# A Mamba block and a mixture of experts on one core: scans 1024 wide in SBUF, the carried state as a leading column, lighter norms, three more PSUM banks, and the order of the work as a written list

## The chip, the core and the metric

The kernel runs on one core of one Trainium2 chip. A core has five engines with a queue each: PE (TensorE, matrix products into PSUM), DVE (VectorE), ACT (ScalarE), POOL (GpSimd) and SP (SyncE, which only issues DMAs here). They work side by side and wait for one another by semaphores. SBUF is the working memory of 128 partitions; PSUM has eight banks of 2 KB per partition, and PE writes only there. POOL can't reach PSUM. The metric is the device time of one execution in microseconds.

## What is computed

The input x has 4 sequences of 512 tokens with 256 channels. Cut to what matters:

```python
x = x + layernorm(mamba(layernorm(x)))
x = x + layernorm(moe(layernorm(x)))

# mamba: 512 inner channels, 16 states each
xs, gate = split(h @ in_proj.T)
xt = silu(conv4(xs) + conv_b)                    # causal, per channel
ts, B, C = split(xt @ x_proj.T)
dt = softplus(ts @ dt_proj.T + dt_b)
for t in range(512):                             # per sequence
    state = state * exp(dt[t] * A) + dt[t] * B[t] * xt[t]
    y[t] = (state * C[t]).sum(states)
out = ((y + xt * D) * silu(gate)) @ out_proj.T

# moe: a shared part of 512 and 16 experts of 128 hidden channels; weights of the top 4
cw = top4(softmax(h @ w_router)), made to sum to 1
moe = sum over e of cw[e] * (silu(h @ we1[e]) * (h @ we3[e])) @ we2[e]
out = shared / 5 + moe * 4 / 5
```

All is float32.

## The kernel before, in words

**Tiling.** The tokens are worked on in units of U = 256, so there are 8 units, two to a sequence (`UB` = 2). Even units begin a sequence, odd units go on with the state that the even one left in the tile `carry`.

**The Mamba part of a unit.** `front` (L655) makes the norm, the transposition, the input product, the convolution (by matmuls), B and C, dt and u = dt * xt, and the gate. dt and u go to DRAM and come back by DMA as `rep` so that a partition holds one (channel, state) pair: 32 channels times 4 states fill 128 partitions, CG = 4 groups of channels make 128 channels (a c of 4), SG = 4 groups of states make 16. B and C come back as `bt` and `ct`. The recurrence runs in slots, numbered by k; a slot handles NJ = 2 groups of channels of one (c, g), 512 columns, so that a unit has 32 slots (`SLOTS`) and the kernel 256:

- `exps` (L523, ACT): two activations of 256 columns write exp(dt * A) into a PSUM tile `h` of one bank (three banks rotate); a copy from `zero` (L532) clears the first column of the second group, so that one scan can run through both without carrying state over.
- `inputs_of` (L534, POOL): `dbx` = u * B, 1024 columns for two slots at once (L541). In odd units a small addition (L543) puts the carried state times the first decay into the first column of each group; that term comes from `decay0` (POOL, L811), `decay1` (ACT, L814) and `delta` (POOL, L818).
- `scan` (L820, DVE): `tensor_tensor_scan` over 512 columns (L824), from `h` (PSUM) and `dbx` (SBUF) into `h`.
- `times_c` (L828, DVE): `hc` = h * C into SBUF (L832), a ring of 11.
- `keep` (L834, ACT): in even units the last column of each group is copied into `carry` (L836).
- `sum_y` (L838, PE): matmuls with `sel` sum over states into the PSUM tile `y`, four slots at a time; `close` (DVE, L858) and `gated_y` (POOL, L864) finish y.

**The expert part of a unit.** `chain` (L918) makes the output product, the norms, the residual and the routing weights. `experts` (L1129) goes through 10 blocks of two experts (the shared part counts as four): `hidden` (PE, L1088) twice into the PSUM tiles `h1` and `h3`, `act` (ACT, L1095 to L1100), `gated` (DVE, L1107, from th in SBUF and h3 in PSUM), `weighted` and `product` (POOL, L1103 and L1110, both operands in SBUF), `down` (PE, L1123, into `po`). The profile shows the PSUM tiles h, h1 and h3 all as "h".

**Norms.** `stats_of` (L374) is one `bn_stats` on DVE; `rstd_of` (L380) is four small POOL instructions (L383 to L386); `normalize` (L389) is two ACT instructions.

**PSUM.** Eight banks: three for the states h, and one each for f, y, h1, h3 and po.

**The order of the work.** Every step is added as a task to `Plan` with an engine, a planned duration, a rank, its dependencies and the buffers that it takes and uses. `Plan.order` (L212) simulates the engines' queues and picks at each point the task that can start soonest, or one of lower rank within the task's patience. SHIFTS, PATIENCE and NUDGES move ranks. The list that comes out is the order in which each engine's queue, SP's DMAs too, is filled. Where PE would idle before the first `down`, `warm` (L346) fills it with products of `ident` (L349).

Of the kernel before, what the change touches and what calls it, by code (L numbers as in the profile page):

```python
# [14 lines left out]
P = 128  # L15
# [19 lines left out]
NJ = 2  # L35
CP = CG // NJ
CSL = SG * CP
SLOTS = CI * CSL
YS = 2 * CP
# [11 lines left out]
    tail=4, bt=2, ct=2, xg=2, rep=3, delta=3, h=3, dbx=3, hc=11, yg=2, o=1, xn2=1, xn_t2=2, lg=2,  # L51
    cw=2, cw_t=1, w13=3, w2=4, cwb=4, th=2, g=3, q=2, res=1, f=1, y=1, h1=1, h3=1, po=1,
# [4 lines left out]
SHIFTS = dict(  # L57
    fA=(-2, -14.75, -1.5, -59.5, 52, 5.75, 37.75, 15),
    fB=(20.5, -5, 12.5, 6.25, 26.25, 45.25, 0, -46),
    fC=(7.75, 2, -31, -1.5, 13.5, 14, -33.5, 18),  # L60
    fD=(12, 34.75, 16.5, 0.25, -2.5, 39.25, 8, 11.25),
    exps=(5.75, 36.5, 17.25, -3.75, -60, 51.75, 2, 37.75),
    dbx=(6.5, 1.25, -27.75, -13.5, -14.25, 5.25, 14.25, 46.5),
    scan=(33.75, 18.75, -5.75, 40.75, 52.75, 51.5, 57.25, -15.75),
    hc=(-4.75, -60, 50.25, -27, 28.5, 59.25, 16.75, 26.75),
    keep=(58, 0, -5.75, 0, 52, 0, 14.5, 0),
    sum=(60, -12.75, 1.25, 31.25, 16.5, 7, 0.5, -43.25),
    close=(-4.75, 27.5, 5.5, -13.75, -3, 20, 15, 36.5),
    ld=(1.5, 29.25, 27, -3, 15.75, -7.5, 57.5, -5.25),
    bc=(5, 3, 5.25, 6, 10.5, 15.75, 0.75, -3.25),  # L70
    chain=(-26, -5.25, -55, -60, -6, -38.25, -22.75, 0.25),
    load=(-5.5, 34, -50.25, 21.25, -21.25, -44, 2.75, 5.5),
    h1=(45.5, 3, -35.75, 8.25, 25.75, -0.5, 14.75, 34.5),
    h3=(11.25, -3, -53.5, -26, -29.25, -19, -15.75, -4),
    act=(-6.25, 40.25, 5.5, -11.5, -31.5, 0, 0, -3.25),
    gated=(-2, -9.5, -4.5, -23.25, 11.75, -60, -3, 0),
    prod=(33, -50, 58.75, -60, -50.75, -26.25, -8.75, 0),
    down=(-18.75, 25.5, -45, 42.25, -60, -14, 0.75, 37),
    fin=(14.75, -3, 27.75, 59, 0.5, 59.5, 3.5, -4),
)  # L80

PATIENCE = dict(
    fA=(1.5, 0.1, 0.1, 0.3, 0.1, 1, 0.3, 0.1),
    fB=(2.2, 0.1, 0.1, 0.3, 0.1, 2.2, 0.6, 0.6),
    fC=(0.3, 0.1, 0.3, 1, 0.1, 0.6, 0.3, 0.3),
    fD=(2.2, 0.1, 0.1, 0.1, 0.1, 0.1, 0.1, 0.6),
    exps=(0.1, 0.1, 0.6, 0.1, 1.5, 0.3, 1.5, 0.3),
    dbx=(0.1, 0.3, 0.1, 0.1, 0.1, 0.1, 1, 1.5),
    scan=(0.1, 0.1, 0.1, 0.6, 0.1, 0.1, 0.1, 0.1),
    hc=(0.1, 0.1, 0.6, 1.5, 2.2, 0.1, 2.2, 0.1),  # L90
    keep=(0.1, 0.1, 0.1, 0.1, 0.6, 0.1, 0.1, 0.1),
    sum=(2.2, 0.1, 0.1, 0.1, 2.2, 0.1, 0.1, 0.1),
    close=(0.1, 0.1, 0.6, 1, 0.3, 0.3, 0.6, 1.5),
    ld=(1.5, 0.3, 1.5, 0.3, 0.1, 0.1, 0.1, 1.5),
    bc=(0.6, 0.1, 0.1, 1, 1, 0.1, 0.1, 0.3),
    chain=(0.6, 0.6, 0.1, 0.6, 0.6, 1, 0.1, 2.2),
    load=(2.2, 1, 0.6, 1, 2.2, 2.2, 0.6, 0.1),
    h1=(0.3, 0.3, 0.3, 0.1, 0.1, 0.1, 0.3, 0.1),
    h3=(0.1, 0.3, 2.2, 0.1, 0.1, 1, 0.6, 0.1),
    act=(0.6, 2.2, 0.1, 0.3, 0.1, 0.1, 0.6, 2.2),  # L100
    gated=(0.6, 0.3, 1, 0.1, 0.6, 0.1, 0.1, 1),
    prod=(2.2, 0.1, 0.1, 0.1, 0.1, 0.3, 0.1, 1.5),
    down=(0.1, 0.1, 0.1, 1.5, 0.1, 0.3, 0.1, 0.3),
    fin=(0.3, 0.3, 0.1, 1.5, 0.1, 1, 1, 0.3),
)

NUDGES = {
    ("gin", 0, 0): 5.5, ("pad0", 1, 0): 5.75, ("in", 1, 0): 3, ("xg", 1, 0, 1): 8,
    ("inputs", 1, 0): 8, ("gate", 1, 0): 14.5, ("evict", 2): 16.5, ("conv", 2, 1): -5.5,
    ("inputs", 2, 0): -27.75, ("pad0", 3, 1): -8, ("conv", 3, 1): 19.25, ("silu", 3, 1): -21.25,  # L110
    ("conv", 4, 0): 25, ("xg", 4, 0, 1): 7.5, ("gin", 4, 1): -27, ("gsig", 4, 1): 18.25,
    ("gate", 4, 1): 9.75, ("x_proj", 5): -1, ("in", 6, 1): -19.75, ("stats", 7): 5.5,
    ("conv", 7, 1): -22.5, ("x_proj", 7): 9.5, ("gin", 7, 0): 12.5, ("dbx", 2): -10,
    ("keep", 6): -14.25, ("keep", 9): -3, ("hc", 11): -1.75, ("keep", 11): -2.5,
    ("keep", 13): 13, ("dbx", 8): 32.75, ("keep", 16): -12, ("keep", 20): -21.25,
    ("scan", 21): 7, ("close", 6): -6, ("decay0", 7): -5, ("sum", 14): -3, ("yg", 7): -0.5,
    ("reps", 10): 12.5, ("hc", 84): 12.75, ("exps", 95): 10, ("exps", 96): -6.25,
    ("scan", 99): -7.75, ("sum", 24): -3, ("decay0", 13): 9.5, ("scan", 106): -3,
    ("sum", 27): -10, ("scan", 112): -14.75, ("scan", 118): 62, ("scan", 122): -3.5,
    ("scan", 125): -6.25, ("scan", 126): 2, ("scan", 138): -8.75, ("keep", 140): -4.75,  # L120
    ("scan", 144): 2.25, ("keep", 146): 27.25, ("scan", 157): 5.75, ("scan", 162): 23.25,
    ("dbx", 84): -4.75, ("decay0", 22): 4.5, ("scan", 179): 53.75, ("dbx", 91): 8.75,
    ("yg", 22): 57, ("scan", 196): -17.5, ("scan", 201): -0.25, ("reps", 26): 6,
    ("scan", 210): 11.25, ("scan", 214): -9, ("scan", 217): 6, ("sum", 54): 3.25,
    ("dbx", 110): -13, ("scan", 223): -8, ("delta", 28): 8.5, ("yg", 28): 24.5,
    ("scan", 235): -2.75, ("close", 29): 8, ("scan", 246): 48.75, ("scan", 252): -1.25,
    ("out0", 0): 35.5, ("rstd2", 0): -27.5, ("w13", 2): -3.75, ("cwb", 2): 15.75,
    ("h3", 3): 26.5, ("w13", 5): 14.75, ("product", 5): -7, ("w2", 6): -15, ("w13", 7): 4,
    ("gated", 7): -2, ("cwb", 9): 19, ("frstd", 0): -20.75, ("fadd", 0): 9.75,
    ("turnw", 1): 8.25, ("w13", 10): -12, ("h1", 10): 11.5, ("act", 15): -17.75,  # L130
    ("weighted", 17): -31.75, ("h3", 18): 3, ("down", 25): 17.75, ("cwb", 26): 10.75,
    ("down", 28): -9, ("h1", 29): -12.75, ("h1", 31): 8, ("down", 33): -14.5,
    ("act", 37): 15.25, ("add1", 4): 13.5, ("act", 46): -14.5, ("w13", 48): 9.5,
    ("share", 5): -10.75, ("cwb", 53): -4, ("h3", 54): 19, ("cwb", 54): -27.5,
    ("down", 54): -5.75, ("w2", 55): 2, ("h1", 55): -5, ("w2", 56): 2.5, ("w2", 58): 16,
    ("cwb", 59): -7.25, ("add1", 6): 8, ("down", 63): 15, ("h1", 67): -13.5, ("h1", 79): 3.25,
    ("fstats", 7, 1): -5, ("fadd", 7, 0): 8.75,
}

GROUPS = dict(  # L140
    fA=(1, "x stats rstd norm transpose evict"),
    fB=(1, "pad0 in tail conv sigmoid silu xg0"),
    fC=(1, "x_proj ssm store_bc dt softplus inputs rep"),
    fD=(1, "gin gsig gate xg1"),
    exps=(SLOTS, "exps"),
    dbx=(SLOTS // CP, "dbx"),
    scan=(SLOTS, "scan"),
    hc=(SLOTS, "hc"),
    keep=(SLOTS, "keep"),
    sum=(SLOTS // YS, "sum"),  # L150
    close=(CI, "close yg"),
    ld=(CI, "reps loadxg decay0 decay1 delta"),
    bc=(1, "bc"),
    chain=(1, "xr out0 out stats1 rstd1 norm1 add1 stats2 rstd2 norm2 turn2 evict2 router pads logits "
           "exp choose chosen total share turnw weigh store_cw"),
    load=(NB, "w13 w2 cwb"),
    h1=(NB, "h1"),
    h3=(NB, "h3"),
    act=(NB, "act"),
    gated=(NB, "gated"),  # L160
    prod=(NB, "weighted product"),
    down=(NB, "down down2"),
    fin=(1, "fin fstats frstd fmean fnorm fadd fstore"),
)
GROUP_OF = {kind: (g, per) for g, (per, kinds) in GROUPS.items() for kind in kinds.split()}


def shift_of(name):
    kind = name[0] + str(name[2]) if name[0] == "xg" else name[0]
    g, per = GROUP_OF[kind]  # L170
    n = name[1] // per
    return SHIFTS[g][n] if g in SHIFTS else 0.0, PATIENCE[g][n] if g in PATIENCE else 0.1


class Plan:
# [22 lines left out]
    def add(self, name, eng, dur, rank, fn, deps=(), alloc=(), uses=(), kb=0, done=None):  # L198
        shift, patience = shift_of(name)
        rank += shift + NUDGES.get(name, 0.0)  # L200
        t = dict(
            name=name, eng=eng, dur=dur, rank=rank, fn=fn, deps=[self.names[d] for d in deps],
            alloc=alloc, kb=kb, done=done, at=len(self.tasks), patience=patience,
        )
        assert name not in self.names, name
        self.names[name] = t
        self.tasks.append(t)
        for key in [key for _, key in alloc] + list(uses):
            self.users.setdefault(key, []).append(t)
        return t  # L210

    def order(self):  # L212
# [4 lines left out]
        for t in self.tasks:  # L217
            waits[t["at"]] = len(t["deps"])
            for d in t["deps"]:
                after.setdefault(d["at"], []).append(t)  # L220
# [1105 lines left out]
```

## Time and profile before

| | |
|---|---|
| runs (3) | median 693.96 us, 693.79 to 693.98 |
| profiled execution: its span, first to last instruction | 692.5 us; the runs' median is 1.4 us longer, which is what lies around the span |
| granted TensorE clock, mean | 0.998 |
| exp, line L529 on ACT | 512 of 478 ns, 244.6 us |
| small POOL instructions of the norms, L383, L384, L385, L386 | 30 each, of 192, 221, 711 and 195 ns |
| clearing a column, L532 on ACT | 256 of 163 ns |
| keep, L836 on ACT | 128 of 159 ns |
| first and last hidden product, L1088 | 120.2 and 681.9 us |
| PE busy with warming, L349, to 30 us and from 30 to 120 us | 11.8 and 19.2 us |

How to read it: "busy" is the time in which an engine has an instruction; the last instruction's end minus the first's start is the span. A line of the groups names the kernel's line, the engine, the operation, out<-in with shapes, how often, then busy microseconds and the mean nanoseconds of one, then the engine's idle time just before them and what ended it. PE's ends are modelled, and a float32 product is recorded as two matmuls. In a stage table the numbers after the stage's length are the busy time and, in brackets, the instructions of each engine.

### The profile page before, as it was taken

Reading aid. Unit: us, or ns where it says so; the run is one execution under the profiler, and the core shown is the slowest. Engines: PE = TensorE matmul, PEld = TensorE weight load, DVE = VectorE, ACT = ScalarE, POOL = GpSimd, SP = SyncE. Lnnn points to the kernel's source line nnn. Section 1 sums busy time; section 2 is a strip of 40 time slices with the busy share of each in tenths; the row PEclk is TensorE's granted clock in tenths of the full one; section 3 lists DMA queues with packets and bytes.
Section 4 is the critical chain, followed back from the end, with each engine's and each line's share of the span. In section 5 each row is a group of like instructions: output and inputs, shape, how many; then the busy total and the mean of one; then the engine's idle time right before and its main releaser. Section 6 shows DMA issues by size and latency. Waiting matters only on the chain.

```text
span 692.5 us, 13366 instructions
## 1 busy us (share of the span) xinstructions
PE 675.8 (98%) x4480; PEld 539.9 (78%) x4480; DVE 578.2 (83%) x821; ACT 493.2 (71%) x1308; POOL 601.6 (87%) x607
## 2 busy tenths in 40 slices
PE   8999998999999999999999999999999999999997
PEld 7777776767878678877787787787877787888886
DVE  3698999999999899999999999889999979952112
ACT  2799979988778778877798857877778657733311
POOL 1598669999999999999999999999999999985553
PEclk9999999999999999999999999999999999999999
DMA  5396775586876586788668766688767756464560
GB/s 175 114 352 227 258 238 188 188 270 202 288 230 226 208 307 207 233 264 285 211 227 281 244 221 229 213 290 286 246 240 232 237 190 213 140 227 128 191 229 31
DMA packets 84840, 155.28 MB, mean 224 GB/s; under 512 B 9858, under 2 KB 33410, under 8 KB 84772
## 3 DMA queue, kind: packets, MB, share of 16 engines
q1 hardware_dynamic: 83940, 153.13, 66.3%
q10 hardware_dynamic: 832, 1.31, 0.5%
q8 instruction: 35, 0.57, 0.3%
q14 instruction: 33, 0.27, 0.1%
HBM read 135.40 MB, written 19.01 MB: 223 GB/s over the span
## 4 chain that ended last, share of the span: by engine, by line
PE 62%; DVE 13%; ACT 10%; POOL 8%; DMA 3%; issue 3%; SPq 0%; DVEq 0%; POOLq 0%
PE h L1088 30%; PE po L1123 14%; DVE h L824 7%; PE y L846 6%; POOL dbx L541 4%; ACT h L529 4%; DVE hc L832 3%; PE f L941 3%; PE f L427 2%; PE f L442 2%; DMA xg<-gate 1%; PE f L1123 1%; PE f L349 1%; DVE gate L786 1%; POOL g L1110 1%
## 5 line engine op out<-in xcount | busy, mean ns | idle before, releaser
L824 DVE TENSOR_TENSOR_SCAN h<-h,dbx 128x512 f32<-128x512 f32 x256 | 307.5, 1220 | 11.5 <-ACT h L532 5.9
L541 POOL TENSOR_TENSOR dbx<-rep,bt 128x1024 f32<-128x1024 f32 x127 | 299.7, 2362 | 12.8 <-DVE h L824 12.5
L1088 PE MATMUL h<-xn_t,w 128*128 128x256 f32 x1280 | 295.2, 382 | 0.1
L529 ACT ACTIVATE h<-rep,a_rep 128x256 f32<-128x256 f32 x512 | 244.6, 478 | 53.4 <-DVE hc L832 41.8
L1088 PEld LDWEIGHTS h<-xn_t,w 128*128 128x128 f32 x1280 | 239.5, 190 | 42.7 <-issue 4.0
L832 DVE TENSOR_TENSOR hc<-h,ct 128x512 f32<-128x512 f32 x256 | 170.2, 682 | 2.9 <-ACT carry L836 0.7
L1123 PE MATMUL po<-w,g 128*128 128x256 f32 x600 | 143.6, 382 | 0.8 <-POOL g L1110 0.8
L1123 PEld LDWEIGHTS po<-w,g 128*128 128x128 f32 x600 | 111.8, 190 | 22.0 <-POOL g L1110 3.2
L1110 POOL TENSOR_TENSOR g<-g,q 128x512 f32<-128x512 f32 x80 | 101.6, 1270 | 9.1 <-DVE q L1107 7.1
L1107 DVE SCALAR_TENSOR_TENSOR q<-th,h 128x512 f32<-128x512 f32 x80 | 54.4, 681 | 49.5 <-PE h L1088 41.6
L1103 POOL TENSOR_TENSOR g<-g,cwb 128x512 f32<-128x512 f32 x64 | 81.4, 1271 | 14.6 <-ACT g L1100 13.9
L1095 ACT ACTIVATE th<-h 128x512 f32<-128x512 f32 x80 | 47.5, 594 | 46.8 <-PE h L1088 46.6
L846 PE MATMUL y<-hc,sel 128*32 128x256 f32 x1024 | 67.7, 385 | 0.0
L846 PEld LDWEIGHTS y<-hc,sel 128*32 128x32 f32 x1024 | 27.4, 109 | 28.6 <-issue 14.5
L532 ACT COPY h<-zero 128x1 f32<-128x1 f32 x256 | 41.7, 163 | 8.2
L427 PE MATMUL f<-xn_t,w_in 128*128 128x256 f32 x176 | 42.5, 384 | 1.6 <-DVE gate L786 1.1
L1100 ACT COPY g<-h 128x512 f32<-128x512 f32 x64 | 37.1, 580 | 8.7 <-PE f L1123 8.7
L427 PEld LDWEIGHTS f<-xn_t,w_in 128*128 128x128 f32 x176 | 32.7, 190 | 9.1 <-DVE gate L786 1.7
L836 ACT COPY carry<-h 128x2 f32<-128x2 f32 x128 | 19.6, 159 | 15.4 <-DVE hc L832 7.7
L442 PE MATMUL h<-xp,taps 64*64 64x256 f32 x288 | 29.5, 381 | 0.8 <-DVE xt L459 0.8
L941 PE MATMUL f<-w_out,yg 128*128 128x256 f32 x112 | 26.7, 384 | 0.3 <-DVE xt L459 0.3
L442 PE MATMUL f<-xp,taps 64*64 64x256 f32 x208 | 25.3, 382 | 0.7 <-DVE gate L786 0.4
(178 smaller groups left out, 631.2 us busy)
## 6 DMA issues: line engine op xcount, KB each, us to landing
w<-in_w SPq DMA_DIRECT2D x80, 512.0 KB, 4.4
rep<-rep SPq DMA_DIRECT2D x124, 256.0 KB, 4.6
w<-in_w SPq DMA_DIRECT2D x80, 256.0 KB, 4.5
cwb<-cwd SPq DMA_DIRECT2D x64, 256.0 KB, 5.1
xg<-xg SPq DMA_DIRECT2D x32, 256.0 KB, 4.5
bt<-bc SPq DMA_DIRECT2D x8, 512.0 KB, 5.8
ct<-bc SPq DMA_DIRECT2D x8, 512.0 KB, 6.1
xg<-gate SPq DMA_DIRECT2D x16, 256.0 KB, 4.6
```

The source lines that it names most:

```text
L427: T.matmul(t[:, j, :], w_in[:, k, ts(2 * m + j, P)], q["xn_t", n][:, k, :], start=k == 0, stop=k == CD - 1,)
L442: T.matmul(t[j][half[r ^ j], :], taps[half[r], 2 * m + j, k, :], q["pad", n, m][half[r], j, k : k + U], start=k == 0, stop=k == KC - 1,)
L529: S.activation(h[:, j, :], dt[:, m, 0, :], AF.Exp, scale=a_rep[:, c, g, m : m + 1])
L541: G.tensor_tensor(t[:, m], reps[n * CI + c][:, m, 1, :], bt[:, m], ALU.mult)
L824: V.tensor_tensor_scan(flat, flat, dbx[:, ts(p, NJ), :].rearrange("p j t -> p (j t)"), 0.0, ALU.mult, ALU.add)
L832: V.tensor_tensor(hc, expo[k], ct, ALU.mult)
L846: T.matmul(ys[n, c][m * CS : (m + 1) * CS, :], sel, hcs[k][:, j, :], start=g == 0, stop=g == SG - 1,)
L1088: T.matmul(t[:, j, :], weights[i][:, j, ts(CD * w + k, P)], x[:, k, :], start=k == 0, stop=k == CD - 1,)
L1103: G.tensor_tensor(gs[i], gs[i], cws[i], ALU.mult)
L1107: V.scalar_tensor_tensor(t, hid[i, "th"], 1.0, hid[i, 1], ALU.add, ALU.mult)
L1110: G.tensor_tensor(gs[i], gs[i], hid[i, "q"], ALU.mult)
L1123: T.matmul(acc[n][t] if n == N - 1 else acc[n][:, t, :], gs[i][:, j, ts(t, P)], weights2[i][:, j, :], start=m == 0 and j == 0 and (t == 0 ...
```

## The change

- NJ goes from 2 to 4: a slot is 1024 columns, 128 slots in all, one `dbx` to a slot. `exps` makes four activations of 256 columns.
- `h` and `dbx` are SBUF tiles (`states`), of 4 x 256 columns in even units and 4 x 257 in odd ones. In odd units the leading column of `h` is zero and that of `dbx` is the carried state, which ACT copies from `carry` (`lead`); the scan then passes it on by itself. `decay0`, `decay1`, `delta` and the addition L543 go. One copy from `zeros` sets the columns of a whole slot.
- `times_c` writes over `h`; the ring `hc` goes, the ring `h` has 6 tiles. So `keep` has to be done before `times_c` in even units. `sum_y` reads `h`.
- The very first scan is made in two parts; `first` makes one slot ahead instead of two.
- Norms: two of the four small POOL instructions become two DVE `tensor_scalar` behind `bn_stats`.
- PSUM: the three banks of h become second banks of f, h1 and h3. The ring cwb goes from 4 to 3.
- SHIFTS, PATIENCE, NUDGES, GROUPS and the choice in `Plan.order` go; a written list ORDER of task numbers gives the order. `Plan.order` still times it, for the amount of warming.

```diff
-NJ = 2
+NJ = 4
+UL = U + 1
...
-    tail=4, bt=2, ct=2, xg=2, rep=3, delta=3, h=3, dbx=3, hc=11, yg=2, o=1, xn2=1, xn_t2=2, lg=2,
-    cw=2, cw_t=1, w13=3, w2=4, cwb=4, th=2, g=3, q=2, res=1, f=1, y=1, h1=1, h3=1, po=1,
+    tail=4, bt=2, ct=2, xg=2, rep=3, h=6, dbx=3, yg=2, o=1, xn2=1, xn_t2=2, lg=2,
+    cw=2, cw_t=1, w13=3, w2=4, cwb=3, th=2, g=3, q=2, res=1, f=2, y=1, h1=2, h3=2, po=1,
...
+        out = [t for t in self.tasks if t["done"] is not None] + [self.tasks[i] for i in ORDER]
...
-    def stats_of(t):
+    def stats_of(t, eps=EPS):
...
         V.bn_stats(st.rearrange("p i k -> p (i k)"), t.rearrange("p i d -> p d i"))
+        V.tensor_scalar(st[:, :, 2], st[:, :, 2], 1.0 / D, eps, ALU.mult, ALU.add)
+        V.tensor_scalar(st[:, :, 1], st[:, :, 1], -1.0, None, ALU.mult)
         return st
...
-        G.tensor_scalar(rstd, st[:, :, 2], 1.0 / D, eps, ALU.mult, ALU.add)
-        G.tensor_scalar(off, st[:, :, 1], -1.0, None, ALU.mult)
-        G.tensor_tensor(rstd, rstd, mhalf, ALU.pow)
-        G.tensor_tensor(off, off, rstd, ALU.mult)
+        G.tensor_tensor(rstd, st[:, :, 2], mhalf, ALU.pow)
+        G.tensor_tensor(off, st[:, :, 1], rstd, ALU.mult)
...
+    def states(nm, n):
+
+        t = work.tile([P, NJ * UL], F32, name=nm, bufs=RINGS[nm])
+        w = U + n % UB
+        return t[:, 0 : NJ * w].rearrange("p (j t) -> p j t", t=w)
+
     def exps(k):
         n, c, g, p = place(k)
-        h = expo[k] = ps_e.tile([P, NJ, U], F32, name="h")
+        h = expo[k] = states("h", n)
+        lead = n % UB
         dt = reps[n * CI + c]
-        for j in range(NJ):
-            m = NJ * p + j
-            S.activation(h[:, j, :], dt[:, m, 0, :], AF.Exp, scale=a_rep[:, c, g, m : m + 1])
-
-        for j in range(1, NJ):
-            S.copy(h[:, j, 0:1], zero)
+        for m in range(NJ):
+            S.activation(h[:, m, lead:], dt[:, m, 0, :], AF.Exp, scale=a_rep[:, c, g, m : m + 1])
+        S.copy(h[:, 1 - lead :, 0], zeros[:, 1 - lead :])
...
-            G.tensor_tensor(t[:, m], reps[n * CI + c][:, m, 1, :], bt[:, m], ALU.mult)
-        if n % UB:
-            G.tensor_tensor(t[:, :, 0], t[:, :, 0], deltas[n * CI + c][:, g, :], ALU.add)
+            G.tensor_tensor(t[:, m, n % UB :], reps[n * CI + c][:, m, 1, :], bt[:, m], ALU.mult)
+
+    def lead(k):
+        n, c, g, p = place(k)
+        S.copy(dbxs[k][:, :, 0], carry[:, c, g, :])
...
     def times_c(k):
         n, c, g, p = place(k)
-        hc = hcs[k] = ring(work, [P, NJ, U], "hc")
         ct = live[n]["ct"][:, g, :].unsqueeze(1).to_broadcast([P, NJ, U])
-        V.tensor_tensor(hc, expo[k], ct, ALU.mult)
+        h = expo[k][:, :, n % UB :]
+        V.tensor_tensor(h, h, ct, ALU.mult)
```

## The prediction

> **What bounds the kernel now.** I read the page's head and its 40 slices, then a table by stage, then the groups and the ranges of the two lines that change most. Head, slices and chain:
>
> ```profile
> span 692.5 us, 13366 instructions
> PE 675.8 (98%) x4480; PEld 539.9 (78%) x4480; DVE 578.2 (83%) x821; ACT 493.2 (71%) x1308; POOL 601.6 (87%) x607
> ...
> PE   8999998999999999999999999999999999999997
> ...
> DVE  3698999999999899999999999889999979952112
> ...
> POOL 1598669999999999999999999999999999985553
> ...
> PE 62%; DVE 13%; ACT 10%; POOL 8%; DMA 3%; issue 3%; SPq 0%; DVEq 0%; POOLq 0%
> ```
>
> PE is busy everywhere, but DVE and POOL are at nine tenths beside it until slice 36. The table by stage, from the first scan (28 us) to the last sum of y (619 us), gives the numbers for the sum:
>
> ```profile
> core 0: us, PE busy (x) PEld busy (x) DVE busy (x) ACT busy (x) POOL busy (x), PEclk, DMA share, GB/s
> 28.00:619.00 591.00, 581.48 (x3959) 458.30 (x3958) 552.33 (x752) 462.94 (x1250) 559.16 (x549) 1.00 0.71 237
> 619.00:692.50 73.50, 68.51 (x324) 59.87 (x322) 14.38 (x33) 18.28 (x36) 38.11 (x45) 0.98 0.45 150
> ```
>
> In these 591 us DVE is busy for 552 and POOL for 559: three engines are nearly full at once, and whatever takes time from DVE or POOL is paid almost at once. PE's busy time has modelled ends, so I count its work: 24 matmul instructions of the hidden products run in 5.18 us in the chain, 0.216 each; y's run 32 in 1.86 us, 0.058 each. Between 120 and 620 us, lines L1088, L1123, L427 and L941 have 1834 instructions (396 us), L846 872 (51 us), the other lines 40 us by their busy time: 487 of 500 us. PE has 13 us to give there, no more. Ahead of it (30 to 120 us) DVE is busy for 86.1 of 90 us while PE fills 19 us with idle warming (L349): there DVE is the bound.
>
> ```profile
> L824 DVE TENSOR_TENSOR_SCAN h<-h,dbx 128x512 f32<-128x512 f32 x256 | 307.5, 1220 | 11.5 <-ACT h L532 5.9
> L541 POOL TENSOR_TENSOR dbx<-rep,bt 128x1024 f32<-128x1024 f32 x127 | 299.7, 2362 | 12.8 <-DVE h L824 12.5
> ...
> L832 DVE TENSOR_TENSOR hc<-h,ct 128x512 f32<-128x512 f32 x256 | 170.2, 682 | 2.9 <-ACT carry L836 0.7
> ...
> L1110 POOL TENSOR_TENSOR g<-g,q 128x512 f32<-128x512 f32 x80 | 101.6, 1270 | 9.1 <-DVE q L1107 7.1
> ```
>
> Shortest, median and longest time of the two big ones, by line:
>
> ```profile
> L824 DVE TENSOR_TENSOR_SCAN h<-h,dbx x256: 1202/1221/1232, 27.9 to 612.2; 128x512 f32<-128x512 f32 x128
> L541 POOL TENSOR_TENSOR dbx<-rep,bt x127: 2347/2361/2386, 29.4 to 608.2; 128x1024 f32<-128x1024 f32 x127
> ```
>
> No scan is over 1% longer than the median and no dbx over 1.1%, though both engines run side by side all the time: **today they do not disturb each other**. But today each of DVE's scans and products has one operand in SBUF (dbx, ct) and one in PSUM (h), while POOL has both operands in SBUF.
>
> **The change part by part.**
>
> Fixed part of a DVE instruction, from two copies out of PSUM:
>
> ```profile
> L610 DVE COPY rep<-f 128x512 f32<-128x512 f32 x1 | 0.7, 692 | 1.2 <-PE f L607 1.2
> ...
> L561 DVE COPY xn_t<-h 128x256 f32<-128x256 f32 x1 | 0.4, 424 | 1.5 <-PE h L560 1.5
> ```
>
> 268 ns for 256 columns is 1.05 ns each, which leaves 156 ns. A scan of 1024 is then 2x1220-156 = 2284 ns, a product 2x682-156 = 1208 ns; 128 of each are 447 us. The 256 pairs of now sum to 256x1.902 = 487 us, of which 478 count as busy because neighbours overlap; I take the saving as 478-447 = 31 us. By itself that is time saved on a full engine.
>
> h moves to SBUF, so scan and product read **both operands from SBUF**. No row of this trace shows a DVE instruction of any size that does so beside a busy POOL. The nearest rows with two SBUF operands are POOL's: (2362-1270)/512 = 2.13 ns per column, twice DVE's 1.05, which is what a path that fetches one operand at a time costs; L832, with one operand from each memory, has DVE's single price ((682-156)/512 = 1.03). Ends: below, nothing (they run side by side as now); above, DVE's 447 us and POOL's work exclude one another. I take the upper end, since the only rows with two SBUF operands are of one fetch after another, so a second SBUF stream of DVE's has to come from somewhere that POOL's row fills; but it is a choice between ends far apart, and both stay in the range.
>
> The Trainium skill, page "SBUF — State Buffer", section "Who interferes with whom", says that a DVE instruction with two SBUF inputs contends with a GpSimd (POOL) instruction that reads SBUF, and that the first to issue holds the shared pair for its whole instruction. It speaks against this change; the undisturbed rows above agree with its other half (one SBUF input, no contention), and no row tests the half that matters. By the rule the sum is that of the forecast, without it that of the first rival.
>
> POOL in the stretch: 559.2, less the carry lines L543 12.9, L811 3.7, L818 3.5, less the norms' L383 5.2 and L384 6.0: 527.9 us, all but 1 us of it with operands in SBUF. DVE gets two small instructions per norm instead, 27x2 of about 0.17 (a 128x2 reciprocal, L1019, takes 0.167): 9 us.
>
> ACT: exp now writes SBUF. Nearest rows: 466 ns (L450, PSUM to SBUF) and 591 (L391, SBUF to SBUF, two per-partition operands) for 478 now: -6 to +58 us over 512; 20 taken. Zeroing 256 to 128 copies: -21; keep 128 to 64: -10; decay1 -3.5; lead +10 (64x0.16). ACT has 128 us idle in the stretch, which hides all of it; in the stretch's tightest cover, 30 to 120 us, it is busy 79.6 of 90, and 5 us could show.
>
> Two new waits. The product overwrites h, so in the first half of each sequence it waits for keep (ACT, 0.16 us, behind at most one exp of 0.48): 64 times 0.16 to 0.64, 10 to 41 us of DVE if no other DVE instruction stands between, nothing if one does; behind it stand q, close and gate, and PE waits for those. I take nothing in a sum where DVE waits for POOL anyway. The scan waits for lead, a copy whose source is from 16 scans before: nothing, unless ACT's queue is late (5.9 us now by L824's releaser).
>
> More banks for f, h1 and h3: at best PE's 13 us. The written order moves all queues, SP's and POOL's among them; its instructions and DMAs are the same except those above; taken as 0, ends -13 us (PE's slack) and +10. A cwb ring of 3 for 4: 5.1 us to land against 2x2.5 us of POOL work each, nothing. Issues of DMAs stay as they are.
>
> **Sum.** If DVE's 447 and POOL's 528 us take turns, the stretch is 975 us instead of 591: +384. Beside one another can still lie the fixed parts: 256x0.156 = 40 of DVE, 399 POOL instructions x 0.18 (2x1271-2362) = 72; all of them: +272. Not covered may be DVE's other work, 552-478+9 = 83 us, which fits into POOL's turns but will not always: all of it: +467. So +272 to +467; with half of the fixed parts hidden and a quarter of the other work not, +384-56+21 = **+349**. 692.5+349 = 1041.5, and 1.4 around the span (median 693.96 against 692.5): **1043 us**. The last 73.5 us stay: POOL is half idle there, and PE is the bound.
>
> **Rivals.**
>
> First, **they do not disturb each other**, on the other side. Then DVE and POOL fall to 552-31+9 = 530 and 528 us, both below PE's work, and PE stays the bound: the gain is what DVE gives before 120 us (83 scans and products merged in pairs, 41x0.156 = 6.4, less 1.3 for norms: 5) and half of PE's 13: 694-5-6.5 = **683 us**, 676 with all of the slack, 692 with a fifth. It decides if a scan keeps 2.28 us and dbx 2.36. For it: the two rows without scatter; against it: that those rows have one SBUF operand.
>
> Second, **they share by the word**, not by the instruction. At one word per 1.05 ns POOL's 528-72 = 456 us need 448 (two words per 2.13 ns) and DVE's second operands 128x2x1024x1.05 ns = 275: 723 us instead of 591, **826 us**. If DVE alone paid POOL's price for the product (2.13 ns a column, 2.34 us), DVE would have 128x(2.28+2.34)+83 = 674: 778 us. Range of this case 700 to 960.
>
> Third, the written order or the keep wait costs more than the rest gives, with undisturbed engines: 696 to 735 us, the 41 us above.
>
> **Chances.** Turns 0.58 (966 to 1162, 1043 likeliest, mostly 966 to 1130); sharing by the word 0.18; undisturbed 0.20, of it 0.18 faster and 0.02 within 0.2%; the third 0.04. So faster 0.18, same 0.02, slower 0.80 (0.2%, 1.4 us, is about what a measurement tells from no change). Without the undisturbed case over 2 in 10 would be left out, so the range reaches from 680, in the middle of that case, to 1130; the forecast's own is 966 to 1130.
>
> **What would show it.** Turns: scan rows far over 2.28 us or dbx rows over 2.36, with a wide scatter; POOL and DVE busy together far over what is summed here; PE with long gaps between 120 us and the end, its hidden products still 0.216 each; the last 73 us as now. Sharing: both rows longer, each with little scatter. Undisturbed: 2.28 and 2.36 to the per cent, and PE's work filling 120 us to the end. Wrong in any case would be the forecast if ACT became the bound (exps over 0.9 us) or if DVE idled before the products (keep).

## The result and the profile after

The changed kernel takes **1025.7 us** in the median of 5 runs (1022.97 to 1026.24); the kernel before takes 693.98 us in 5 (693.79 to 694.43). The ratio is 1.477 [1.475, 1.479], 332 us more. The prediction had 1043 us for its likeliest case, turns between DVE and POOL.

The page of the changed kernel: span and busy times, the busy tenths of PE, DVE and POOL in 40 slices, and the engines' shares of the chain of waits.

```profile
span 1022.7 us, 12684 instructions
PE 772.2 (76%) x4428; PEld 593.8 (58%) x4428; DVE 835.4 (82%) x628; ACT 445.5 (44%) x1164; POOL 923.7 (90%) x451
...
PE   9775776976777786676766686767687776788997
...
DVE  3999998889898979799798998789798899676211
...
POOL 0899898999999999999899999999999999897364
...
POOL 45%; PE 19%; issue 15%; DVE 14%; ACT 3%; DMA 3%; SPq 0%; POOLq 0%; DVEq 0%; ACTq 0%
```

POOL has taken PE's place: 45% of the chain for 8% before, and nines, but for two eights, from slice 8 to slice 36. The instruction counts show what is odd in that. POOL has 451 instructions for 607 and DVE 628 for 821, and yet POOL is busy for 923.7 us instead of 601.6 and DVE for 835.4 instead of 578.2. So the instructions have become longer.

The table by stage, from the first scan to the last sum of y and from there to the end:

```profile
core 0: us, PE busy (x) PEld busy (x) DVE busy (x) ACT busy (x) POOL busy (x), PEclk, DMA share, GB/s
28.00:946.00 918.00, 674.91 (x3893) 509.28 (x3892) 807.81 (x551) 415.58 (x1106) 883.06 (x399) 0.85 0.46 153
946.00:1022.70 76.70, 71.36 (x338) 62.51 (x336) 16.00 (x40) 17.85 (x35) 36.08 (x39) 0.99 0.43 138
```

The first stage has grown from 591 to 918 us, the last from 73.5 to 76.7. In the first, POOL is busy for 883 of 918 us, with work that the prediction counted at 528 us: by that count 355 us of it are no work. The timeline below shows of what kind they are.

The groups of the page that matter most (busy and mean of one, then the idle time before them):

```profile
L806 DVE TENSOR_TENSOR_SCAN h<-h,dbx 128x1024 f32<-128x1024 f32 (+2 forms) x129 | 409.7, 3192 | 52.0 <-POOL dbx L533 33.7
L533 POOL TENSOR_TENSOR dbx<-rep,bt 128x1024 f32<-128x1024 f32 x127 | 409.5, 3235 | 9.1 <-DVE h L806 8.9
...
L1088 POOL TENSOR_TENSOR g<-g,q 128x512 f32<-128x512 f32 x80 | 171.8, 2151 | 17.5 <-DVE q L1085 16.0
...
L1085 DVE SCALAR_TENSOR_TENSOR q<-th,h 128x512 f32<-128x512 f32 x80 | 53.4, 673 | 55.8 <-PE h L1066 43.3
```

The POOL product at L1088 is the untouched one that took 1270 ns before; it now takes 2151 in the mean. The DVE product at L1085 was not touched either and keeps its time (673 ns): it has one operand in SBUF (th) and one in PSUM (the bank of h3, shown as h). Shortest, median and longest time of scan, POOL product and DVE product:

```profile
L806 DVE TENSOR_TENSOR_SCAN h<-h,dbx x129: 1683/3181/6860, 27.5 to 925.5; 128x1028 f32<-128x1028 f32 x64, 128x1024 f32<-128x1024 f32 x63, 128x512 f32<-128x512 f32 x2
...
L533 POOL TENSOR_TENSOR dbx<-rep,bt x127: 2328/3329/4471, 30.0 to 913.2; 128x1024 f32<-128x1024 f32 x127
...
L814 DVE TENSOR_TENSOR h<-h,ct x128: 1193/2220/3437, 36.5 to 934.0; 128x1024 f32<-128x1024 f32 x128
```

This is the scatter that was named as the mark of turns. The shortest dbx (2328) and the shortest product (1193) have the undisturbed lengths, the longest are about two to three times as long. The shortest alone do not exclude a division word by word, since they may have met an idle engine; the timeline that follows and the pairs further down do.

One scan in the timeline of the changed kernel (start, length, engine, line; in brackets the idle time before):

```profile
500.55 2.35 POOL L533 TENSOR_TENSOR dbx<-rep,bt 128x1024 f32<-128x1024 f32 x1
...
502.86 1.26 POOL L1081 TENSOR_TENSOR g<-g,cwb 128x512 f32<-128x512 f32 x1
...
502.93 6.86 DVE L806 TENSOR_TENSOR_SCAN h<-h,dbx 128x1024 f32<-128x1024 f32 x1 [2.33 <-POOL dbx L533]
...
504.08 2.34 POOL L533 TENSOR_TENSOR dbx<-rep,bt 128x1024 f32<-128x1024 f32 x1
...
506.38 1.26 POOL L1088 TENSOR_TENSOR g<-g,q 128x512 f32<-128x512 f32 x1
```

The scan starts 0.07 us after L1081. It is recorded as busy until 509.79, but the three POOL instructions that run meanwhile (L1081, L533, L1088) have their undisturbed lengths and end at 507.64; 2.15 us are left for the scan, near the 2.28 of an undisturbed one. Had the two engines shared by the word, POOL's three would have been longer. So the wait stands inside the duration, and no view of waits shows it: the scan looks as if it worked for 6.86 us.

### The profile page after: what moved, and what is told of

The parts are those of the page before. It is cut to its first block, busy times and chain, and to the rows that moved or that the text cites. A ratio compares the mean times of both kernels' runs of the same rounds, so it can differ in the third digit from the quotient of the medians.

```text
span 1022.7 us, 12684 instructions
## 1 busy us (share of the span) xinstructions
PE 772.2 (76%) x4428; PEld 593.8 (58%) x4428; DVE 835.4 (82%) x628; ACT 445.5 (44%) x1164; POOL 923.7 (90%) x451
## 4 chain that ended last, share of the span: by engine, by line
POOL 45%; PE 19%; issue 15%; DVE 14%; ACT 3%; DMA 3%; SPq 0%; POOLq 0%; DVEq 0%; ACTq 0%
POOL dbx L533 16%; POOL g L1088 10%; POOL g L1081 8%; DVE h L806 7%; PE h L1066 7%; PE po L1101 6%; DVE h L814 4%; POOL rstd L373 3%; POOL yg L846 2%; POOL u L748 2%; ACT h L523 2%; POOL off L374 1%; POOL xr L935 1%; PE y L828 1%; DMA w<-in_w 1%
## 5 line engine op out<-in xcount | busy, mean ns | idle before, releaser
L806 DVE TENSOR_TENSOR_SCAN h<-h,dbx 128x1024 f32<-128x1024 f32 (+2 forms) x129 | 409.7, 3192 | 52.0 <-POOL dbx L533 33.7
L533 POOL TENSOR_TENSOR dbx<-rep,bt 128x1024 f32<-128x1024 f32 x127 | 409.5, 3235 | 9.1 <-DVE h L806 8.9
L814 DVE TENSOR_TENSOR h<-h,ct 128x1024 f32<-128x1024 f32 x128 | 286.3, 2253 | 2.1 <-ACT carry L818 2.0
L1101 PE MATMUL po<-w,g 128*128 128x256 f32 x600 | 191.7, 476 | 119.0 <-POOL g L1088 108.3
L1101 PEld LDWEIGHTS po<-w,g 128*128 128x128 f32 x600 | 138.6, 238 | 158.4 <-POOL g L1088 121.8
L1088 POOL TENSOR_TENSOR g<-g,q 128x512 f32<-128x512 f32 x80 | 171.8, 2151 | 17.5 <-DVE q L1085 16.0
L1081 POOL TENSOR_TENSOR g<-g,cwb 128x512 f32<-128x512 f32 x64 | 127.6, 1996 | 14.1 <-ACT g L1078 12.3
L828 PE MATMUL y<-h,sel 128*32 128x256 f32 x1024 | 76.8, 424 | 39.4 <-DVE h L814 30.2
L1085 DVE SCALAR_TENSOR_TENSOR q<-th,h 128x512 f32<-128x512 f32 x80 | 53.4, 673 | 55.8 <-PE h L1066 43.3
L828 PEld LDWEIGHTS y<-h,sel 128*32 128x32 f32 x1024 | 28.9, 117 | 77.7 <-DVE h L814 38.5
L373 POOL TENSOR_TENSOR rstd<-st,mhalf 128x2 f32<-128x2 f32 x30 | 50.3, 1677 | 8.4 <-DVE st L367 8.0
L846 POOL TENSOR_TENSOR yg<-xg 128x256 f32<-128x256 f32 x32 | 50.9, 1590 | 6.2 <-DVE xg L840 6.2
```

Of the source, the lines that this page charges most:

```text
L373: G.tensor_tensor(rstd, st[:, :, 2], mhalf, ALU.pow)
L533: G.tensor_tensor(t[:, m, n % UB :], reps[n * CI + c][:, m, 1, :], bt[:, m], ALU.mult)
L806: V.tensor_tensor_scan(flat, flat, dbx[:, m, :].rearrange("p j t -> p (j t)"), 0.0, ALU.mult, ALU.add)
L814: V.tensor_tensor(h, h, ct, ALU.mult)
L828: T.matmul(ys[n, c][m * CS : (m + 1) * CS, :], sel, expo[k][:, j, n % UB :], start=g == 0, stop=g == SG - 1,)
L846: G.tensor_tensor(ygs[n, c // 2][:, c % 2, :], xg[:, 0, :], xg[:, 1, :], ALU.mult)
```

## The experiments

Theory T: DVE and POOL take turns, instruction by instruction, wherever DVE reads two operands from SBUF. Its rivals: the written order and its waits cost the time; it is what is written into SBUF that counts; the lighter norms cost nothing. The kernel before took 694.0 to 694.5 us beside these runs. Times without an interval are of a single run, which is enough for differences of 100 us and more.

**A base for three runs: the kernel before with a smaller ring.** The tiles in SBUF need room, which a ring hc of 8 for 11 makes.

```diff
-    ... h=3, dbx=3, hc=11, ...
+    ... h=3, dbx=3, hc=8, ...
```

> The kernel before with a ring of 8 instead of 11 product tiles hc, which also changes the order that the planner writes. It is the base for the next three, which need the room in SBUF. Turns: 694 us give or take 10, scan 1.22 and dbx 2.36 us without scatter. The rival that the loss lies in the order or in smaller rings: something of it shows here, over 720 us.

Measured: 717.78 us, so the expectation was wrong by 24 us: the smaller ring, with the other order that the planner makes of it, costs 3.4%. The scans stay at 1203/1222/1232 ns and dbx at 2345/2362/2391, without scatter. The next three runs are read against 717.8.

**Only the memory of h: PSUM to SBUF**, with scans still 512 wide, the planner's order and the norms as before.

```diff
-    ps_e = ctx.enter_context(tc.tile_pool(name="ps_e", bufs=RINGS["h"], space=PSUM))
+    ps_e = ctx.enter_context(tc.tile_pool(name="ps_e", bufs=RINGS["h"]))
```

> The kernel before (ring hc of 8) with one edit: the states h lie in SBUF instead of PSUM. Scans stay 512 wide, the order, the carry and the norms stay. Turns (a DVE instruction with two SBUF operands and a POOL instruction exclude one another): DVE's 487 us of scans and products and POOL's 559 us, times 0.94 as in the changed kernel (918 us for 975), are 983 us instead of 591: 1088 us, 1020 to 1110; scan, product and dbx rows scatter up to several us. Rival, the loss comes from the width, the written order or the carry's column: 690 to 720 us, rows without scatter.

Measured: 1057.64 us, 340 more than the base, from taking away one argument. The ranges of scan, product and POOL's product in this run:

```profile
L824 DVE TENSOR_TENSOR_SCAN h<-h,dbx x256: 1191/1453/3385, 27.5 to 974.8; 128x512 f32<-128x512 f32 x128
...
L832 DVE TENSOR_TENSOR hc<-h,ct x256: 658/1152/2889, 31.0 to 977.6; 128x512 f32<-128x512 f32 x128
...
L541 POOL TENSOR_TENSOR dbx<-rep,bt x127: 2338/2798/3329, 29.9 to 964.9; 128x1024 f32<-128x1024 f32 x127
```

The same scatter at half the width, without the written order, the leading column or the new norms: the memory of h brings it about alone.

**Reading or writing, scan or product.** Two runs divide the two roles of h: exp in PSUM and the scan's output in SBUF (only the product reads two SBUF operands), and exp in SBUF with the scan's output in PSUM (only the scan reads two).

```diff
+    ps_o = ctx.enter_context(tc.tile_pool(name="ps_o", bufs=RINGS["h"]))
...
+        to = expo[k] = ps_o.tile([P, NJ, U], F32, name="hs")
...
-            flat, flat, dbx[:, ts(p, NJ), :].rearrange("p j t -> p (j t)"), 0.0, ALU.mult, ALU.add
+            to.rearrange("p j t -> p (j t)"), flat,
+            dbx[:, ts(p, NJ), :].rearrange("p j t -> p (j t)"), 0.0, ALU.mult, ALU.add
```

In the second run the pools have their memories exchanged:

```diff
-    ps_e = ctx.enter_context(tc.tile_pool(name="ps_e", bufs=RINGS["h"], space=PSUM))
+    ps_e = ctx.enter_context(tc.tile_pool(name="ps_e", bufs=RINGS["h"]))
+    ps_o = ctx.enter_context(tc.tile_pool(name="ps_o", bufs=RINGS["h"], space=PSUM))
```

> The kernel before (ring hc of 8), exp still into PSUM, but the scan writes to a tile in SBUF: the scan has one SBUF operand and an SBUF output, the product has two SBUF operands. Turns by what is read: scan rows stay at 1.22 us without scatter, product rows scatter; 175 us of products and POOL's 559 take turns, 734 times 0.94 is 690 instead of 591: 794 us, 760 to 840. Rival, writes into SBUF collide with POOL too: the scan rows scatter as well, over 950 us. Rival, no turns: 694.

> The kernel before (ring hc of 8), exp into SBUF, the scan reads both operands from SBUF and writes to PSUM, the product reads one from PSUM and one from SBUF. Turns by what is read: product rows stay at 0.68 us without scatter, scan and dbx rows scatter; 312 us of scans and POOL's 559 take turns, 871 times 0.94 is 819 instead of 591: 923 us, 880 to 960. Rival, writes into SBUF are what collides: 694 us, no scatter.

Measured: 864.82 us with the product alone on two SBUF operands, 927.04 us with the scan alone. Scan and product with the scan's output in SBUF:

```profile
L826 DVE TENSOR_TENSOR_SCAN hs<-h,dbx x256: 1189/1209/1225, 27.1 to 782.7; 128x512 f32<-128x512 f32 x128
...
L835 DVE TENSOR_TENSOR hc<-hs,ct x256: 657/1166/2873, 29.3 to 786.3; 128x512 f32<-128x512 f32 x128
```

The same with exp in SBUF:

```profile
L826 DVE TENSOR_TENSOR_SCAN hs<-h,dbx x256: 1199/1732/3422, 27.4 to 843.3; 128x512 f32<-128x512 f32 x128
...
L835 DVE TENSOR_TENSOR hc<-hs,ct x256: 666/677/693, 30.9 to 846.4; 128x512 f32<-128x512 f32 x128
```

The scatter changes sides with the operand that is read: the scan that writes SBUF and reads one PSUM operand is as even as before, so writing does not count and reading does. The two losses over the base, 147 and 209 us, add up to 356, near the 340 of both together. The first expectation was too low by 71 us in its middle. It counted the product's turns only; a likely reason, which no run tests by itself, is that a product that waits in DVE's queue holds back the scans behind it. In that run's chain of waits the undisturbed scans stand with 22% and the products with 18%, and DVE is 87% busy.

**The changed kernel with one operand in PSUM, and its control.** A PSUM bank of the constant 0.5 stands for the decay in the scan and for C in the product; h1 gives up its second bank for it, and entries of the list that would need that bank are moved back. The control has the same order and the same bank and keeps both operands in SBUF.

```diff
-                flat, flat,
+                flat, fixed[:, 0:1].to_broadcast(list(flat.shape)),
...
-        V.tensor_tensor(h, h, ct, ALU.mult)
+        V.tensor_tensor(h, h, half, ALU.mult)
```

> The changed kernel with one of the two operands of each scan and product read from a constant bank of PSUM instead of from SBUF: 0.5 takes the place of exp(dt*A) in the scan and of C in the product (this leaves out the decay and C; exp and the load of C still run). The bank comes from the ring h1 (1 instead of 2), and the written order is made legal for it by moving a task behind what it must wait for. All else of the change stays: SBUF states, 1024 columns, lead, keep, norms, written order. Turns: scans at 2.2 to 2.3 us and products at 1.2, both without scatter, dbx at 2.36, and the time of the forecast's first rival, 683 us, 676 to 720 with one bank less. Rival, the order, the waits or the width cost something: far over 720 us.

> The control for the run with a constant PSUM operand: the same order and the same h1 ring of 1, but the changed kernel's own operands, both in SBUF. Turns: 1026 us give or take 25, rows scattered as in the changed kernel. Rival, the bank or the order made the difference: below 900 us.

Measured: 726.22 us with one operand in PSUM (4 runs; ratio to the kernel before 1.046 [1.044, 1.048]); the control takes 1026.72 us. Scan, product and POOL's product of the first:

```profile
L834 DVE TENSOR_TENSOR_SCAN h<-fixed,dbx x129: 1198/2283/2300, 27.1 to 625.8; 128x1028 f32<-128x1028 f32 x64, 128x1024 f32<-128x1024 f32 x63, 128x512 f32<-128x512 f32 x2
...
L843 DVE TENSOR_TENSOR h<-h,fixed x128: 1186/1208/1222, 34.4 to 631.7; 128x1024 f32<-128x1024 f32 x128
...
L561 POOL TENSOR_TENSOR dbx<-rep,bt x127: 2339/2375/2439, 28.6 to 614.2; 128x1024 f32<-128x1024 f32 x127
```

The scatter is gone (POOL's longest is within 3% of its median), and the medians are those that the prediction worked out from two copies: 2284 and 1208 ns. The control differs in nothing but the two operands, so having both in SBUF costs 1026.7 - 726.2 = 300.5 us. (With constants for them the scan and the product also no longer need the values of exp and C; exp is still made, and the scan still waits for its tile, 17.2 us for the column's clearing against 25.1 in the control.) The expected 683 us (676 to 720) was too low; the next runs look for the rest.

**Pairs, measured by themselves.** Twelve DVE and twelve POOL instructions of 128x512 run alone and side by side, in eight stages.

```diff
+    def two_sbuf():
+        V.tensor_tensor(dv, a, b, ALU.mult)
+    def beside_two_sbuf():
+        G.tensor_tensor(po, ga, gb, ALU.mult)
+    def one_psum():
+        V.tensor_tensor(dv, bank, b, ALU.mult)
```

> No part of the computation: stages of 12 DVE and 12 POOL instructions side by side, all 128x512 unless told. Stages: DVE alone (product of two SBUF tiles); POOL alone (product of two SBUF tiles); both; DVE with one operand in PSUM beside POOL; DVE with two in SBUF beside a POOL memset; a DVE scan with two in SBUF beside POOL; a DVE tensor_scalar SBUF to SBUF beside POOL; the same of 128x2. Turns by what is read: alone 0.68 and 1.27 us; both: one of the two stretches to the sum, about 1.8 us a pair; one operand in PSUM: 0.68 and 1.27, no scatter; memset: no stretch; scan: about 2.4 us a pair. Rival, any two SBUF accesses: the memset and the PSUM stage stretch too. The tensor_scalar stages are open: stretched if one SBUF input is enough for a wide mode, else 0.3 to 0.7 and 0.17.

The timeline of this run: start and length of twelve instructions, first each engine alone, then both on SBUF, then DVE with one PSUM operand beside the same POOL product, then a DVE scan of two SBUF operands beside it:

```profile
5.43 8.68 DVE L39 TENSOR_TENSOR dv<-a,b 128x512 f32<-128x512 f32 x12 [4.03 <-ACT st L90]
...
16.64 16.00 POOL L42 TENSOR_TENSOR po<-ga,gb 128x512 f32<-128x512 f32 x12 [13.04 <-ACT st L90]
...
34.38 19.03 DVE L45 TENSOR_TENSOR dv<-a,b 128x512 f32<-128x512 f32 x12 [20.27 <-ACT gb L89]
34.58 19.94 POOL L48 TENSOR_TENSOR po<-ga,gb 128x512 f32<-128x512 f32 x12 [1.94 <-ACT st L90]
...
56.26 8.67 DVE L51 TENSOR_TENSOR dv<-bank,b 128x512 f32<-128x512 f32 x12 [2.86 <-ACT gb L89]
56.47 16.03 POOL L54 TENSOR_TENSOR po<-ga,gb 128x512 f32<-128x512 f32 x12 [1.94 <-ACT st L90]
...
85.22 24.73 DVE L63 TENSOR_TENSOR_SCAN dv<-a,b 128x512 f32<-128x512 f32 x12 [2.31 <-ACT gb L89]
85.43 25.58 POOL L66 TENSOR_TENSOR po<-ga,gb 128x512 f32<-128x512 f32 x12 [4.10 <-ACT st L90]
```

Alone 8.68 and 16.00 us; with one PSUM operand 8.67 and 16.03 side by side, so nothing is lost. With two SBUF operands POOL's twelve end after 19.94 us: not the 24.7 us of strict turns, but 81% of it, so 4.7 us, or 0.40 for a pair, still lie beside one another. The fixed parts of the prediction, 0.156 and 0.18 us, are most of that. So a pair takes 1.66 us, less than the 1.8 expected.

The scan beside POOL settles the rival of sharing by the word. Both engines read as many words there as in the stage with the products, so sharing would have kept POOL's twelve near 19.9 us; they take 25.6, or 2.13 for a pair (2.4 were expected). A DVE scan is 0.53 us longer than a DVE product (shortest ones 1.225 and 0.693 us), and each of POOL's untouched products is longer by 0.47 (medians 2.059 and 1.588). Each waits for the whole of the other engine's instruction, but for some 0.4 us.

A POOL memset, which reads nothing, leaves DVE at 8.68 us. And an instruction with a single SBUF operand waits as well: a tensor_scalar of 128x512 takes 1.29 us in the mean beside POOL (its shortest 0.43), and one of 128x2 takes 0.64 (0.17). That puts the lighter norms in question.

**The norms alone**: the kernel before with only the change of `stats_of` and `rstd_of`.

```diff
         V.bn_stats(st.rearrange("p i k -> p (i k)"), t.rearrange("p i d -> p d i"))
+        V.tensor_scalar(st[:, :, 2], st[:, :, 2], 1.0 / D, eps, ALU.mult, ALU.add)
+        V.tensor_scalar(st[:, :, 1], st[:, :, 1], -1.0, None, ALU.mult)
...
-        G.tensor_scalar(rstd, st[:, :, 2], 1.0 / D, eps, ALU.mult, ALU.add)
-        G.tensor_scalar(off, st[:, :, 1], -1.0, None, ALU.mult)
```

> The kernel before with the lighter norms alone: two of four small POOL instructions become two DVE instructions of 128x2 from SBUF to SBUF; order and all else stay. If such a DVE instruction with one SBUF input takes turns with POOL as well (rows of the changed kernel: 0.168 to 2.18 us), 60 of them stretch by some half a microsecond each and the 12 us that POOL gains are given back: 694 to 705 us. Rival, they run at 0.17 us and POOL's 12 us count: 688 to 693 us.

Measured: 711.54 us, 1.026 [1.023, 1.028], more than either side expected. The two new instructions in this run:

```profile
L378 DVE TENSOR_SCALAR st<-st x31: 168/590/1955, 6.5 to 659.7; 128x2 f32<-128x2 f32 x31
...
L379 DVE TENSOR_SCALAR st<-st x31: 154/155/1314, 6.6 to 660.4; 128x2 f32<-128x2 f32 x31
```

Two values per partition take up to 1.96 us. In the trace one L378 starts at 300.89 us, 0.43 after a dbx of POOL's, and ends at 302.85, 0.03 after that dbx: the first waits for POOL's instruction, and the second mostly follows at its own length. DVE is busy for 25 us more and POOL for 11 less, and the kernel, which PE bounds with 13 us of slack, takes 17 us more (694.5 beside this run).

**The norms elsewhere.** Two runs ask whether it is the form of the instruction: the numbers from tiles of one column instead of constants, and the two small steps on ACT. Both edits are shown against the run with the norms alone.

```diff
-        V.tensor_scalar(st[:, :, 2], st[:, :, 2], 1.0 / D, eps, ALU.mult, ALU.add)
-        V.tensor_scalar(st[:, :, 1], st[:, :, 1], -1.0, None, ALU.mult)
+        V.tensor_scalar(st[:, :, 2], st[:, :, 2], numbers[:, 0:1], numbers[:, e : e + 1], ALU.mult, ALU.add)
+        V.tensor_scalar(st[:, :, 1], st[:, :, 1], numbers[:, 1:2], None, ALU.mult)
```

```diff
-        V.tensor_scalar(st[:, :, 2], st[:, :, 2], 1.0 / D, eps, ALU.mult, ALU.add)
-        V.tensor_scalar(st[:, :, 1], st[:, :, 1], -1.0, None, ALU.mult)
+        S.activation(st[:, :, 2], st[:, :, 2], AF.Copy, scale=1.0 / D, bias=eps)
+        S.mul(st[:, :, 1], st[:, :, 1], -1.0)
```

> The kernel before with the lighter norms, whose two small DVE instructions take their numbers from [128,1] tiles instead of from the instruction. In the kernel before a tensor_scalar SBUF to SBUF with numbers in the instruction took 283 ns for 256 columns, one with two such tiles 410, so that form does not run in the wide mode. If only the wide mode takes turns with POOL: small instructions at 0.17 to 0.3 us without scatter, POOL's 12 us saved, 688 to 697 us. Rival, any DVE instruction from SBUF to SBUF waits, or the loss of the lighter norms (711.5 us) lies in the order of the chain: 705 us or more.

> The kernel before with the lighter norms, the two small steps on ACT instead of on DVE. ACT is idle for 29% of the span and takes no part in DVE's and POOL's turns: if those were the loss, 690 to 698 us (each step may stand behind an exp of 0.48 us). Rival, the lighter norms lose by the order of the chain whatever engine does the small steps: 705 us or more.

With tiles of one column 715.75 us, 1.031 [1.030, 1.032], and the first step at 287/582/1949 ns: still scattered, so the first expectation (688 to 697) failed, and why is not settled (the tile of numbers is itself read from SBUF). On ACT 698.07 us, 1.006 [1.004, 1.008]. So some 13 of the 17 us come from the two steps standing on DVE, where the rows show them waiting for POOL. The order of the chain, the rival, leaves at most the other 4; but even so the lighter norms bring nothing here.

**The rest of the changed kernel.** First, one operand in PSUM and POOL's norms as before, which takes the last instructions away that were seen to wait for POOL (the edit is shown against the run with one operand in PSUM).

```diff
-        V.tensor_scalar(st[:, :, 2], st[:, :, 2], 1.0 / D, eps, ALU.mult, ALU.add)
-        V.tensor_scalar(st[:, :, 1], st[:, :, 1], -1.0, None, ALU.mult)
...
+        G.tensor_scalar(rstd, st[:, :, 2], 1.0 / D, eps_of[id(st)], ALU.mult, ALU.add)
+        G.tensor_scalar(off, st[:, :, 1], -1.0, None, ALU.mult)
```

> The changed kernel with one operand of each scan and product from a constant PSUM bank (726 us; decay and C left out as there), and in addition the norms as before, four small POOL instructions. If the lighter norms cost here what they cost the kernel before (17 us): 705 to 715 us. Rival, the rest of the 32 us lies wholly in the order made legal and the missing bank: 722 to 730 us.

Measured: 713.88 us, 1.029 [1.027, 1.031]: the norms cost 12.3 us in this kernel too. In its table of waits PE waits 17.1 us and its weight loads 27.8 us for ACT's g, the reader of h1, which has one bank in this run. So a last one gives h1 its two banks and f only one.

```diff
-    ... f=2, y=1, h1=1, h3=2, ...
+    ... f=1, y=1, h1=2, h3=2, ...
```

> The kernel is one_operand_pool_norms with another bank left out: f has one bank and h1 two, instead of f two and h1 one. As there, the scan's decay and the product's C are the constant 0.5 from a PSUM bank, so that the states are not the reference's. It asks where that run's 19 us over the kernel before come from. If the missing second bank of h1 is the cause (PE waits there 17.1 and 27.8 us for ACT's g, the reader of h1), these waits fall to under 5 us and the time to 690 to 703 us, as long as f's waits do not take their place. If the cause is the written order and the planner's lead over it (PE's start, the last units), the time stays within 708 to 720 us. A middle value would divide the 19 us between the two.

Measured: 736.70 us, 1.059 [1.055, 1.063], outside both expectations. The waits of PE for g are gone, as expected, but others came: ACT's sig waits 27.8 us for PE's h, and POOL's dbx 28.3 us for DVE's scan, for 12.2 in the run before. So the missing bank of f costs 23 us more than that of h1 (the ring hc of 8, with an order planned anew for it, cost 24 above), and these runs can't tell what the written order would give with all its banks and no turns. The 19 us of the run before are thus not divided between bank and order.

**What it adds up to.** Taken away one after the other, 300 of the 332 us belong to the two SBUF operands of scan and product (shown by the control) and about 12 to the lighter norms (12 measured there, 17 in the kernel before). The other 19 us were measured only with a bank missing; their cause stays open. No version beat the kernel before.

## Why the prediction was right

- **Two operands in SBUF.** The choice between ends far apart was the step that decided, and it was right: the engines take turns by the instruction. Its argument from the rows was weaker than the choice. POOL's price of 2.13 ns per column does not tell turns from sharing by the word, for the second rival is worked out from the same figure; and DVE alone reads two SBUF operands at 692 ns for 512 columns, without paying double. Ahead of the runs only the rule of the skill that it names sets the two apart, and no row tested that rule; by the rows alone the choice was partly luck. The Trainium skill, page "SBUF — State Buffer", section "Who interferes with whom", speaks of what DVE reads and of POOL instructions that read, and the runs agree on both: the scan that reads one SBUF operand and writes SBUF keeps 1209 ns, and beside a memset DVE's twelve keep 8.68 us.
- **The sum.** 975 us less half of the fixed parts (56) plus a quarter of DVE's other work (21) made a stretch of 940 us; it took 918, inside the ends of 863 and 1058. 975 - 918 = 57 us is just the half of the fixed parts, as if the added 21 us were not needed. That is the error, with 3 us back in the last stage. But it is partly luck: by the 0.40 us that the pairs showed, 256 DVE instructions would have hidden 101 us (an estimate), which would leave 44 us lost elsewhere. No run divides the two.
- **Durations.** 2284 and 1208 ns were computed; 2283 and 1208 were measured where nothing disturbs.
- **Mis-sized: the norms.** Taken were "two small instructions per norm ..., of about 0.17 ... 9 us" for 11.2 us off POOL. Measured were a median of 0.59 us for the first one, and a loss of 12 to 17 us for the edit. The row that gave 0.17 is a reciprocal (L1019, 166/166/167 ns), which does not scatter in the kernel before. A nearer look at the same section of that page would have spoken against it: it counts tensor_scalar among the operations that can enter a two-port mode and so contend with GpSimd, when their operands meet certain conditions. In the trace of before the tensor_scalars on SBUF stand in the first 28 us (taps, L366, 247 ns), where POOL is busy for 4.3 us only, so no row of it tests that; in the runs it scattered, in the changed kernel too (168/479/2180 ns).
- **Rival one was too cheap.** 683 us for the undisturbed case counted the norms as next to no loss; the nearest runs are 714 and 726 us, one bank short. (Its 692 "with a fifth" does not add up either if a fifth of the slack is meant: 694 - 5 - 2.6 is 686.) The sign that this rival stood for was therefore too favourable: without the turns, "faster" was not shown by any run.
- **Waits at nothing.** The product waits 2.0 us for keep (L814's releaser, carry), against 10 to 41 us at the upper end; lead is in no line of waits of the scan. ACT's exps take 499 ns for 478, and ACT is 44% busy and has 3% of the chain: hidden. The last stage has 76.7 us for 73.5.
- **Marks.** Scatter, DVE and POOL far over their sums, PE with gaps (108.3 us of waiting at L1101 for POOL's g, L1088), all as named. Single hidden products keep a median of 380 ns (379 before), though their mean rises from 382 to 399.

## What to carry to other kernels

Before an operand of a DVE instruction moves from PSUM to SBUF, count how many SBUF operands it reads and whether POOL is busy reading beside it: with two, DVE and POOL took turns here, the stretch came near the sum of both engines' times (918 us for 447 + 528), and it cost 300 us, ten times the 31 us that fewer instructions were to save. Where a DVE or POOL row scatters to twice or three times its shortest time, the engine may not be working but waiting inside the instruction; no view of waits shows that, and the timeline of the other engine does. Small instructions count too: a tensor_scalar of 128x2 stood up to 1.96 us behind a product of 1024.

## What the runs showed of the hardware beyond that

- **Turns need not alternate.** In the pairs they did, one for one (after the first, every DVE scan took 2.10 us and every POOL product 2.06). In the changed kernel the scan at 502.93 us waited for the running POOL instruction and then for two more that were issued after it, 4.7 us in all. On the other hand a POOL copy of 128x6 took 2.21 us behind the scan before (L712, 498.38 us). The page named above says that the first to issue holds the pair; by the starts that this timeline records, the next turn did not go to the one that had waited longer. What decides it stays open.
- **PE's granted clock was lower in the runs in which PE was busy for less of the span.** It was 0.866 in the changed kernel (PE busy for 76%; 0.85 in the long stage, 0.99 in the last), 0.886 with h in SBUF (77%), 0.933 and 0.96 in the two halves (82 and 85%), and 0.99 or more in most of the undisturbed runs (93 to 97%; 0.982 at 94% in the last). No run here tests what causes it. PE had room for it: it is busy for 675 of 918 us. With 19% of the chain, the lower clock can account for about 26 of the 1022.7 us (an estimate: 194 us of chain, times 1 - 0.866/0.998).
